# A transformer block on one core: where the row-sum fold, the row inverses and the two norms stand in a hand-written order of slots

## The chip, the cores and the metric

The kernel runs on one core of a Trainium2 chip. A core has a matrix engine (TensorE, PE in the profile; its weight loads are shown as PEld), a vector engine (VectorE, DVE), a scalar engine for activation functions and copies (ScalarE, ACT), a general engine (GpSimd, POOL) and a queue engine that here only issues transfers (SyncE, SP). Each engine works through its own instructions in order and waits for others by semaphores. ScalarE and GpSimd can issue transfers too, from within their own order of instructions. The metric is the time of one execution on the device in microseconds (us), the median of several runs.

## What is computed

The input x is 4 sequences of 1024 tokens with 512 features, with a condition vector of 128 values for each sequence. The block is a transformer layer with normalizations that are scaled and shifted by the condition:

```python
def _tc_rmsnorm(x, t, gw, gb, bw, bb):
    g = (t @ gw.T + gb)[:, None, :]
    b = (t @ bw.T + bb)[:, None, :]
    inv_rms = jax.lax.rsqrt(jnp.mean(x * x, axis=-1, keepdims=True) + EPS)
    return g * x * inv_rms + b
...
y = x + _attention(_tc_rmsnorm(x, t, g1w, g1b, b1w, b1b), Wq, Wk, Wv, Wo)
return x + (y + _swiglu(_tc_rmsnorm(y, t, g2w, g2b, b2w, b2b), gate_w, hid_w, out_w))
```

Attention has 16 heads of 32 features with a softmax over 1024 keys. swiglu is silu(x @ gate_w.T) * (x @ hid_w.T) @ out_w.T with 2048 hidden features. (The last lines put the reference's steps together; the names are the reference's.)

## The kernel before, in words

**Tiles.** Features lie on the 128 partitions (C = 4 chunks), tokens along the free dimension. A block n is 512 tokens (NBLK = 8 blocks; a sequence b is two of them, its halves). Attention is cut into groups j: one block, one chunk of four heads and 256 queries make one group, so a block has 8 groups and there are 64. A group has UN = 4 rounds r of 256 keys each.

**Slots.** Everything is in one loop over slots g, 0 to 267 (L758). A slot's kind is g % 4. Slot g computes the scores of round g (scores(), L301), copies them from PSUM (keep(), L308, tile raw) and takes the running maximum (L313, L316). The later steps of a round follow one group behind: in slot g, shifted() subtracts the row maximum from round g - 5 on VectorE (L354), exponential() follows on ScalarE (L357), and weighted() multiplies round g - 6 with the values on TensorE (L367, tile av), so it needs the exponential of the slot before. Accumulating transfers on GpSimd's queue add up the four rounds of a group for the row sums (L381). At kind 0 the maxima of the group before are transposed (max_T(), tile mt), reduced and split on VectorE (parts(), L328 to L333); at kind 1 they are transposed back (parts_T(), tile pt, then the copy mT on ScalarE, L340) and spread (spread(), L348 and L349, tile shift).

**Row sums and inverses.** fold_sum() (L389) adds the two halves of the accumulated exponentials on VectorE, 128x1024. It stands at the end of the kind 3 slot. sums() (L399) and the copy sums_out() (L404, tile total) follow in the next slot, kind 0. inverse() (L407) and normalize() (L416, which writes the tile oT) stand near the head of that group's kind 2 slot, ahead of shifted(). The product of a block's first group is put off to the kind 1 slot of the next group.

**The feed-forward part** joins at slot FS = 60 and is worked off by units p, one in two slots (p = (g - 60) // 2; 16 units for each block, with seven products of halves in place of eight). In the even slot: pair_26(), copy_156(), the contraction with the output weights of an earlier unit (filler(), tile pc), its addition to the residual take_contract() (L568), pair_7() and sub_5() (L537). In the odd slot: pair_3(), tanh (L547), pair_15() and take_5() (L511) of the next unit, gate() (L552), add_15() (L515), pair_4() and hidden() (L555). pair_26() of the next even slot writes the bank that add_15() has read. Until slot 60, projections for the later sequences (project_kq(), project_v()) fill the slots instead, one or two a slot, handed out by chain() from a queue in order. weight_sums() makes sums of feed-forward weights, four VectorE operations, in each third slot from 6 to 51.

**The norms.** The first norm of half a sequence that comes later: norm_squares() (squares on ScalarE, L132, sums on VectorE, L135 and L138), norm_root() (a matmul with ones over the partitions, tile pma, then the root from PSUM to SBUF, L146), a reciprocal on VectorE (L622), norm_scale() (L184) and norm_mod() (L187) for each chunk. Six of these run in the slots before 60; the root stands in the kind 0 slots 4, 12, 20, 28, 36 and 44. The second norm of block n, with g0 = 32 (n + 1), starts when project_out() (tile po, addition L435) has made x2. Its root is made in slot g0 + 17 on all 128x512 values (in every partition the same 512), and then one row is written to DRAM by norm_compact(), read back as 128x4 by take(), inverted there by invert() (L162), written out by put() and read to all partitions by norm_spread() (L173), which SP issues. compact(), take() and put() are issued by ScalarE. Then come norm_scale(), norm_mod() and token_sums() (L482 to L488), which prepares the sums for the feed-forward products. This goes for blocks 0 to 6; block 7 is normed at the end in another way.

**What sets the order.** The order on PE, DVE, ACT and POOL is the order in which the code calls the steps. SP's issues are ordered by the framework, and SP waits at each issue until its buffer is free. pin(g, ...) puts a load into slot g, between() puts a step near a slot's end (halfway), after() at its very end (ended), amid within an odd slot of the feed-forward part, behind take_5(). Scores use PSUM banks of their own; projections, row sums, means and spreads share two banks of the pool ps (tag w), with a third for each third projection (ps_b); av has its own bank (ps_av).

Of the kernel before, what the change touches and what calls it, by code (L numbers as in the profile page):

```python
# [10 lines left out]
F32 = mybir.dt.float32  # L11
BF16 = mybir.dt.bfloat16
AF = mybir.ActivationFunctionType
# [4 lines left out]
P = 128  # L18
NB = 512
# [5 lines left out]
def tile_cond_transformer_block(  # L25
# [24 lines left out]
    HQ = 256  # L50
# [77 lines left out]
    def norm_squares(dst, tag: str, k: int):  # L128

        sq = [sb.tile([P, NB], F32, tag="t", name=f"sq{tag}_{2 * k + i}", bufs=2) for i in range(2)]  # L130
        for i in range(2):
            nc.scalar.activation(sq[i], dst[:, 2 * k + i, :], AF.Square)  # L132
        if k == 0:
            state[tag] = sb.tile([P, NB], F32, tag="tot", name=f"tot{tag}", bufs=1)
            nc.vector.tensor_tensor(state[tag], sq[0], sq[1], ALU.add)  # L135
        else:
            for t in sq:
                nc.vector.tensor_tensor(state[tag], state[tag], t, ALU.add)  # L138

    def norm_root(tag: str, inside: bool = False):  # L140
        if inside:
            pm = ps_av.tile([P, NB], F32, tag="av", name=f"pm{tag}")
        else:
            pm = ps.tile([P, NB], F32, tag="w", name=f"pm{tag}")
        mm(pm, ones_mean, state[tag], True, True)
        nc.scalar.activation(state[tag], pm, AF.Sqrt, bias=eps)  # L146

    def compact(tag: str, t, rows: int, n: int):

        inv_s[tag] = tc.dram_tile([P // rows, n], F32, name=f"sums{tag}")  # L150
        nc.scalar.dma_start(out=inv_s[tag], in_=t[0:P:rows, :])

    def take(tag: str):

        src = inv_s.pop(tag)
        few = sb.tile([P, src.shape[0] * src.shape[1] // P], F32, tag="few", name=f"few{tag}", bufs=2)
        nc.scalar.dma_start(out=few, in_=src.rearrange("h (p c) -> (h p) c", c=few.shape[1]))
        state["few", tag] = few

    def invert(tag: str):  # L160
        few = state["few", tag]
# [2 lines left out]
    def put(tag: str):  # L164
        few = state.pop(("few", tag))
        inv_s[tag] = tc.dram_tile(list(few.shape), F32, name=f"invs{tag}")
        nc.scalar.dma_start(out=inv_s[tag], in_=few)

    def spread_inverse(tag: str, t, rows: int, n: int):

# [216 lines left out]
    def fold_sum(j: int):  # L387
        t = acc[j]
        nc.vector.tensor_tensor(t[:, 0, :, :], t[:, 0, :, :], t[:, 1, :, :], ALU.add)  # L389
# [16 lines left out]
    def inverse(j: int):  # L406
        nc.vector.reciprocal(state["total", j], state["total", j])  # L407
# [163 lines left out]


    NR = NBLK * C * (NB // HQ) * UN
    BS = C * (NB // HQ) * UN
    MS = BS // C
    pinned = {}
    first = deque()
# [35 lines left out]
    for b in range(1, B):  # L613
        for half in range(QB):
            s = math.ceil((len(queue) + 1) / PACE)
            s4 = s - 4 - (s - 6) % UN
            tag = f"a{b}_{half}"
            pin(max(s4 - 6, 0), load_y, b, half)
            for k in range(2):
                after(s4 - 4 + k, lambda b=b, half=half, tag=tag, k=k: norm_squares(y[b, half], tag, k))  # L620
            between(s4 - 2, norm_root, tag)
            after(s4 - 1, lambda tag=tag: nc.vector.reciprocal(state[tag], state[tag]))  # L622
            for c in range(C):
                between(s4, lambda b=b, half=half, tag=tag, c=c: norm_scale(y[b, half], tag, c))
                after(s4 + c // 2, lambda b=b, half=half, c=c: norm_mod(0, b, y[b, half], c))
            for load, fn, a in chains_of(b, half):
                enqueue(s, load, fn, a)
# [4 lines left out]
    for n in range(NBLK):  # L632
        g0 = (n + 1) * BS
        pin(g0 + 6, load_res, n)
        go = g0 + (13 if n < NBLK - 1 else 8)
        for d in range(C):
            first.append((go, None, project_out, (n, d)))
            pin(go - 3 + (d // 2 * 4 if n else 0), load_wo, n, d)
        if n < NBLK - 1:
            tag = f"f{n}"  # L640
            after(g0 + 16, add_res, n)
            for k in range(2):
                after(g0 + 15 + k, lambda n=n, tag=tag, k=k: norm_squares(x2[n], tag, k))
            if g0 + 17 < FS:
                between(g0 + 17, norm_root, tag)
            else:
                amid.setdefault(g0 + 17, []).append((norm_root, (tag, True)))
            between(g0 + 17, norm_compact, tag)
            after(g0 + 19, take, tag)
            between(g0 + 20, invert, tag)  # L650
            after(g0 + 21, put, tag)
            after(g0 + 22, norm_spread, tag)
            for c in range(C):
                after(g0 + 24 + c // 2, lambda n=n, tag=tag, c=c: norm_scale(x2[n], tag, c))
            for c in range(2):
                after(g0 + 25, lambda n=n, c=c: norm_mod(1, n // QB, x2[n], c))
            for c in range(2, C):
                between(g0 + 26, lambda n=n, c=c: norm_mod(1, n // QB, x2[n], c))
            for i in range(4):
                after(g0 + (26, 26, 27, 28)[i], token_sums, n, i)  # L660
    for m in range(NBLK * C):
        if m:
            for qh in range(NB // HQ):
# [24 lines left out]
    with tc.manual_schedule(  # L688
# [69 lines left out]
        while g < END:  # L758
# [17 lines left out]
                scores(g)  # L776
            if kind == 1 and m_on:
                spread(j_m, 0)

            if kind == 2 and n_on and j_n < direct:  # L780
                inverse(j_n)
                if j_n % (BS // UN):
                    normalize(j_n)
            if kind == 1 and n_on and j_n % (BS // UN) == 1:
                normalize(j_n - 1)
            if x_on and kind != 1:
                shifted(r_x)
            if late is not None:
# [17 lines left out]
            if not ffn:  # L806
# [20 lines left out]
                    add_15(0)  # L827
                elif even:
                    late = chain(g, FG)
                if kind == 3 and s_on:  # L830
                    fold_sum(j_s)
                if g in (FS - 4, FS - 2):
                    load_f((g - FS + 4) // 2)
            elif even:
# [22 lines left out]
            else:  # L857
# [27 lines left out]
                if kind == 1:  # L885
                    gate(p)
                    if evict is not None:
                        evict()
                if kind == 3 and s_on:
                    fold_sum(j_s)  # L890
                pair_4(p)
                hidden(p)
                if due:
                    chain(g)()
                for fn, a in halfway.pop(g, []):
                    fn(*a)
            columns[0] = DH
            for fn, a in ended.pop(g, []):
                fn(*a)
# [93 lines left out]
```

## Time and profile before

| | |
|---|---|
| time, median of 3 runs | 2498.34 us (2495.81 to 2498.56) |
| the profiled execution's own time | 2495.65 us |
| its span from first to last instruction | 2493.8 us |
| PE busy | 2392.5 us, 96% of the span |
| DVE busy | 1941.8 us, 78% |
| ACT busy | 1406.4 us, 56% |
| transfers | 501.69 MB, mean 201 GB/s |
| slots 0 to 59 | from 50 to 544 us |
| slots 60 to 255 | from 544 us on; slot 254 begins at about 2144 us |

How to read it: the profile shows one execution. A row such as "L354 DVE TENSOR_TENSOR raw<-raw,shift ... x320 | 594.1, 1857 | 101.7" gives the source line, the engine, the operation, what it writes from what, the shapes, how often, its busy time in us, the mean of one in ns, and the idle time of the engine just ahead of it. In a view in order of time, a line begins with its start and its length in us, and what stands in brackets at its end is how long the engine was idle ahead of it and which instruction ended that. In the view of waits a line names who waited for whom, the total in us, how often, and the longest. Matmuls are pipelined, so TensorE counts as busy also while one waits in its pipe; what counts are the gaps and the lengths of slots.

### The profile page before, as it was taken

What the parts mean: (1) busy time and instruction counts of PE and PEld (TensorE: products, weight loads), DVE (VectorE), ACT (ScalarE), POOL (GpSimd) and SP (SyncE); (2) the same over time, 40 slices, a digit from 0 to 9 for tenths busy, and PEclk for the clock granted to TensorE, in tenths of its full rate; (3) what the DMA queues carried; (4) which work ended last, traced back from release to release, by engine and by line L of the source; (5) the groups of instructions that cost most, each with busy time, mean ns of one, the idle gap of its engine ahead of it and who ended that gap; (6) DMA issues with size and microseconds to landing.
All of it is one profiled execution on the core that took longest, in us unless ns stands there. A gap on an engine that the chain in (4) does not pass through costs nothing. (4 is left out here: it accounts for less than half of the span.)

```text
span 2493.8 us, 71084 instructions
## 1 busy us (share of the span) xinstructions
PE 2392.5 (96%) x31749; PEld 1125.5 (45%) x31749; DVE 1941.8 (78%) x2180; ACT 1406.4 (56%) x1488; POOL 172.4 (7%) x207
## 2 busy tenths in 40 slices
PE   8999999999999999999999999999999999999999
PEld 3333333345444444444444444444444444444444
DVE  2688888878979997999789988998899979843332
ACT  3677667766656665666566656665666656522111
POOL 0000000000000000000000000000000000000000
PEclk9999999999999999999999999999999999999999
DMA  6698999888878898888878888889788978863442
GB/s 213 175 290 242 239 250 235 221 209 230 209 174 205 210 229 200 194 207 225 203 186 202 234 191 199 207 214 221 180 204 195 240 183 202 195 177 112 141 131 73
DMA packets 185982, 501.69 MB, mean 201 GB/s; under 512 B 21319, under 2 KB 78663, under 8 KB 158286
## 3 DMA queue, kind: packets, MB, share of 16 engines
q0 software_dynamic: 28656, 208.68, 42.7%
q1 hardware_dynamic: 154704, 288.42, 35.3%
q8 instruction: 250, 4.10, 0.6%
q10 hardware_dynamic: 2318, 0.05, 0.1%
q14 instruction: 54, 0.44, 0.1%
HBM read 246.44 MB, written 41.97 MB: 116 GB/s over the span
## 5 line engine op out<-in xcount | busy, mean ns | idle before, releaser
L354 DVE TENSOR_TENSOR raw<-raw,shift 128x2048 f32<-128x2048 f32 (+1 forms) x320 | 594.1, 1857 | 101.7 <-ACT shift L349 98.2
L357 ACT ACTIVATE raw<-raw 128x2048 f32<-128x2048 f32 x256 | 490.9, 1918 | 321.2 <-DVE raw L354 321.0
L308 ACT COPY raw<-sc 128x2048 f32<-128x2048 f32 x256 | 478.8, 1870 | 86.0 <-PE sc L301 44.0
L313 DVE TENSOR_TENSOR rmax<-rmax,raw 128x1024 f32<-128x1024 f32 x384 | 469.1, 1222 | 58.1 <-ACT raw L308 53.2
L106 PE MATMUL pc<-h,ow 128*32 128x512 f32 x4096 | 467.9, 593 | 2.3 <-ACT total L404 1.1
L367 PE MATMUL av<-raw,v 128*32 128x256 f32 x4096 | 274.1, 385 | 61.5 <-ACT raw L357 55.1
L381 POOL DMA_DIRECT2D raw<-raw x192 | 165.3, 861 | 2009.0 <-ACT raw L357 945.4
L301 PE MATMUL sc<-q,k 32*128 32x256 f32 x4096 | 293.3, 400 | 1.8 <-ACT raw L308 1.8
L106 PE MATMUL pa<-x,fa 128*32 128x256 f32 x4096 | 269.1, 380 | 8.1 <-DVE pa L515 8.0
L106 PE MATMUL pa<-sums,fw 128*32 128x256 f32 x4096 | 267.9, 379 | 0.0
L106 PEld LDWEIGHTS pc<-h,ow 128*32 128x32 f32 x4096 | 127.6, 110 | 246.5 <-issue 221.6
L301 PEld LDWEIGHTS sc<-q,k 32*128 32x128 f32 x4096 | 184.9, 184 | 117.8 <-issue 79.4
L106 PE MATMUL pkq<-y,wkq 128*32 128x512 f32 (+1 forms) x1664 | 231.6, 594 | 4.2 <-ACT y L187 4.1
L367 PEld LDWEIGHTS av<-raw,v 128*32 128x32 f32 x4096 | 106.9, 109 | 188.3 <-ACT raw L357 109.8
L106 PEld LDWEIGHTS pa<-x,fa 128*32 128x32 f32 x4096 | 127.5, 109 | 122.8 <-DVE pa L515 28.8
L106 PEld LDWEIGHTS pa<-sums,fw 128*32 128x32 f32 x4096 | 133.1, 110 | 87.9
L530 ACT COPY pb<-pa 128x256 f32<-128x256 f32 x128 | 46.3, 362 | 179.5 <-PE pa L106 174.9
L547 ACT ACTIVATE t<-pa 128x512 f32<-128x512 f32 x128 | 78.0, 609 | 119.7 <-PE pa L106 119.6
L106 PE MATMUL pa<-x,fw 128*32 128x256 f32 x2048 | 135.2, 381 | 0.0
L106 PE MATMUL pb<-x,fw 128*32 128x256 f32 x2048 | 134.0, 379 | 1.2 <-ACT pb L530 1.2
L106 PE MATMUL pb<-sums,fa 128*32 128x256 f32 x2048 | 134.0, 379 | 0.0
L106 PEld LDWEIGHTS pkq<-y,wkq 128*32 128x32 f32 (+1 forms) x1664 | 73.2, 116 | 131.5 <-issue 119.4
(104 smaller groups left out, 2166.0 us busy)
## 6 DMA issues: line engine op xcount, KB each, us to landing
raw<-raw POOLq DMA_DIRECT2D x192, 1024.0 KB, 9.2
fw<-sw SPq DMA_DIRECT2D x128, 512.0 KB, 5.8
fa<-in_gh_w SPq DMA_DIRECT2D x128, 384.0 KB, 7.8
ow<-in_out_w SPq DMA_DIRECT2D x128, 256.0 KB, 3.4
wkq<-in_kq_w SPq DMA_DIRECT2D x32, 512.0 KB, 9.1
v<-vs SPq DMA_DIRECT2D x128, 128.0 KB, 6.0
k<-kqs SPq DMA_DIRECT2D x124, 128.0 KB, 7.7
kqs<-st SPq DMA_DIRECT2D x61, 256.0 KB, 6.3
```

The source lines that it names most:

```text
L106: nc.tensor.matmul(dst[k : k + n, :], w[:, k : k + n], moving, start=start, stop=stop, skip_group_check=seeded)
L301: nc.tensor.matmul(sc[:, i, k, :], keys[rows, k * P : (k + 1) * P], queries[rows, :], start=True, stop=True)
L308: nc.scalar.copy(raw[r].rearrange("p k h q -> p h k q"), state.pop(("sc", r)))
L313: nc.vector.tensor_tensor(rmax[j], rmax[j], raw[r][:, k, :, :], ALU.max)
L354: nc.vector.tensor_tensor(t, t, s.unsqueeze(1).to_broadcast(list(t.shape)), ALU.add)
L357: nc.scalar.activation(raw[r], raw[r], AF.Exp)
L367: nc.tensor.matmul(av[j][i * DH : (i + 1) * DH, :], v[m, u][:, k, i * DH : (i + 1) * DH], raw[r][:, k, i, :], start=(kt == 0), stop=(kt == ...
L381: nc.gpsimd.dma_start(out=acc[j].rearrange("p k h q -> p (k h q)"), in_=raw[r].rearrange("p k h q -> p (k h q)"), accum_op=ALU.add,)
L530: nc.scalar.copy(bank_b[p][:, RIGHT], bank_a[p][:, RIGHT])
L547: nc.scalar.activation(state["t", p], bank_a[p], AF.Tanh, scale=0.5)
```

## The change

It moves steps to other places in the order; the arithmetic of the results is the same but for where the second norm's root is taken.

- fold_sum() goes from the end of the kind 3 slot to the head of the next slot, kind 0, ahead of shifted() (and so behind hidden() of the slot before).
- inverse() and normalize() go from the head of the kind 2 slot to its end, behind sub_5(). For a block's last group they stand at the end of the kind 0 slot. Only block 1's first product is still put off to kind 1.
- The first norm's load, squares, root and reciprocal come one slot sooner: the root at the end of kind 3, the reciprocal at the end of kind 0. Scaling stays where it was.
- The second norm of blocks 1 to 6 starts four slots sooner, with its output projection (slots g0 + 9 and g0 + 11 for g0 + 13 and g0 + 15) and the loads of its weights. Its mean is copied from PSUM in slot g0 + 13 instead of the root (norm_mean()), goes to DRAM and back as 128x4, and the root is taken there (root(), end of slot g0 + 16), with the inverse at the end of g0 + 17. The scalings stand at the ends of g0 + 22 (two chunks) and g0 + 24, the modulations in g0 + 23 and g0 + 25, the first token sum at the end of g0 + 25. Block 0 keeps its places, with the root at the end of slot 52 and norm_mean() in 49.
- compact(), take() and put() are issued by SP.

```diff
-    def norm_root(tag: str, inside: bool = False):
+    def norm_root(tag: str):
...
+    def norm_mean(tag: str, inside: bool):
...
-        nc.scalar.activation(state[tag], pm, AF.Sqrt, bias=eps)
+        nc.scalar.copy(state[tag], pm)
...
-        nc.scalar.dma_start(out=inv_s[tag], in_=t[0:P:rows, :])
+        nc.sync.dma_start(out=inv_s[tag], in_=t[0:P:rows, :])
...
-        nc.scalar.dma_start(out=few, in_=src.rearrange("h (p c) -> (h p) c", c=few.shape[1]))
+        nc.sync.dma_start(out=few, in_=src.rearrange("h (p c) -> (h p) c", c=few.shape[1]))
...
+    def root(tag: str):
+        few = state["few", tag]
+        nc.scalar.activation(few, few, AF.Sqrt, bias=eps)
...
-        nc.scalar.dma_start(out=inv_s[tag], in_=few)
+        nc.sync.dma_start(out=inv_s[tag], in_=few)
...
-            pin(max(s4 - 6, 0), load_y, b, half)
+            pin(max(s4 - 7, 0), load_y, b, half)
             for k in range(2):
-                after(s4 - 4 + k, lambda b=b, half=half, tag=tag, k=k: norm_squares(y[b, half], tag, k))
-            between(s4 - 2, norm_root, tag)
-            after(s4 - 1, lambda tag=tag: nc.vector.reciprocal(state[tag], state[tag]))
+                after(s4 - 5 + k, lambda b=b, half=half, tag=tag, k=k: norm_squares(y[b, half], tag, k))
+            between(s4 - 3, norm_root, tag)
+            after(s4 - 2, lambda tag=tag: nc.vector.reciprocal(state[tag], state[tag]))
...
-        go = g0 + (13 if n < NBLK - 1 else 8)
+        e = g0 if n == 0 else g0 - 4
+        go = e + 13 if n < NBLK - 1 else g0 + 8
...
-            after(g0 + 16, add_res, n)
+            after(e + 16, add_res, n)
             for k in range(2):
-                after(g0 + 15 + k, lambda n=n, tag=tag, k=k: norm_squares(x2[n], tag, k))
-            if g0 + 17 < FS:
-                between(g0 + 17, norm_root, tag)
+                after(e + 15 + k, lambda n=n, tag=tag, k=k: norm_squares(x2[n], tag, k))
+            if n == 0:
+                between(e + 17, norm_mean, tag, False)
             else:
-                amid.setdefault(g0 + 17, []).append((norm_root, (tag, True)))
-            between(g0 + 17, norm_compact, tag)
-            after(g0 + 19, take, tag)
-            between(g0 + 20, invert, tag)
-            after(g0 + 21, put, tag)
-            after(g0 + 22, norm_spread, tag)
+                amid.setdefault(e + 17, []).append((norm_mean, (tag, True)))
+            after(e + 17, norm_compact, tag)
+            after(e + 19, take, tag)
+            after(e + 20, root, tag)
+            after(e + (20 if n == 0 else 21), invert, tag)
+            after(e + (21 if n == 0 else 22), put, tag)
+            after(e + (22 if n == 0 else 24), norm_spread, tag)
+            scales, mods = ((24, 24, 25, 25), (25, 25, 26, 26)) if n == 0 else ((22, 22, 24, 24), (23, 23, 25, 25))
             for c in range(C):
-                after(g0 + 24 + c // 2, lambda n=n, tag=tag, c=c: norm_scale(x2[n], tag, c))
-            for c in range(2):
-                after(g0 + 25, lambda n=n, c=c: norm_mod(1, n // QB, x2[n], c))
-            for c in range(2, C):
-                between(g0 + 26, lambda n=n, c=c: norm_mod(1, n // QB, x2[n], c))
+                after(g0 + scales[c], lambda n=n, tag=tag, c=c: norm_scale(x2[n], tag, c))
+                between(g0 + mods[c], lambda n=n, c=c: norm_mod(1, n // QB, x2[n], c))
             for i in range(4):
-                after(g0 + (26, 26, 27, 28)[i], token_sums, n, i)
+                after(g0 + (26, 26, 27, 28)[i] - (n > 0 and i == 0), token_sums, n, i)
...
-            if kind == 2 and n_on and j_n < direct:
-                inverse(j_n)
-                if j_n % (BS // UN):
-                    normalize(j_n)
-            if kind == 1 and n_on and j_n % (BS // UN) == 1:
-                normalize(j_n - 1)
+            if kind == 0 and n_on:
+                fold_sum(j_n)
+            if kind == 1 and j_n == GB + 1:
+                normalize(GB)
...
-                if kind == 3 and s_on:
-                    fold_sum(j_s)
...
+            if kind == 0 and n_on and j_n < direct and j_n % GB == GB - 1:
+                inverse(j_n)
+                normalize(j_n)
+            if kind == 2 and n_on and j_n < direct and j_n % GB != GB - 1:
+                inverse(j_n)
+                if j_n != GB:
+                    normalize(j_n)
```

More of the change, by code (lines that the diff above doesn't have):

```diff
@@ L138, in norm_squares @@
                 nc.vector.tensor_tensor(state[tag], state[tag], t, ALU.add)
-    def norm_root(tag: str, inside: bool = False):
+    def norm_root(tag: str):
+        pm = ps.tile([P, NB], F32, tag="w", name=f"pm{tag}")
+        mm(pm, ones_mean, state[tag], True, True)
+        nc.scalar.activation(state[tag], pm, AF.Sqrt, bias=eps)
+    def norm_mean(tag: str, inside: bool):
         if inside:
@@ L573, in tile_cond_transformer_block @@
     NR = NBLK * C * (NB // HQ) * UN
-    BS = C * (NB // HQ) * UN
+    GB = C * (NB // HQ)
+    BS = GB * UN
     MS = BS // C
@@ L888, in tile_cond_transformer_block @@
                         evict()
-                if kind == 3 and s_on:
-                    fold_sum(j_s)
                 pair_4(p)
```

## The prediction, made before the changed kernel was run

> **What bounds the kernel now.** I read the busy times, then who waits for whom on TensorE before and after 544 us (slot 60, where the feed-forward part joins), then stretches of single groups, then the order in time of each engine. Slots, kinds and groups are those explained above: slot g, kind g mod 4, group of four slots.
>
> ```profile
> PE 2392.5 (96%) x31749; PEld 1125.5 (45%) x31749; DVE 1941.8 (78%) x2180; ACT 1406.4 (56%) x1488; POOL 172.4 (7%) x207
> ```
> TensorE is busy nearly throughout. The change removes no matmul, so it can win only TensorE's idle time, some 100 us. Before 544 us, TensorE's own waits are (us in total, times, longest):
> ```profile
> PE av L367 <- ACT raw L357: 17.1, 15, 2.4
> PE pma L106 <- ACT total L404: 7.6, 5, 1.7
> PE sc L301 <- ACT raw L308: 1.8, 3, 1.0
> PE sp L348 <- ACT shift L349: 0.7, 1, 0.7
> ```
> That is 27.2 us in the front. It hangs on the first norm, once per half sequence, as around slots 28 to 30:
> ```profile
> 281.53 1.13 PE L106 MATMUL pma<-tota,ones_mean 128*128 128x512 f32 x2 [1.66 <-ACT total L404]
> ...
> 294.74 1.07 PE L367 MATMUL av<-raw,v 128*32 128x256 f32 x16 [1.30 <-ACT raw L357]
> ```
> ```profile
> 291.49 1.28 ACT L357 ACT_TABLE_LOAD   x1
> ```
> ```profile
> 288.14 2.55 DVE L354 TENSOR_TENSOR raw<-raw,shift 128x1024 f32<-128x1024 f32 x2 [4.96 <-ACT shift L349]
> ...
> 293.63 3.35 DVE L622 RECIPROCAL tota<-tota 128x512 f32<-128x512 f32 x1
> ```
> The mean's matmul waits for the row sums' bank; the root's table must be swapped back just before the exponential that weighted() needs (1.30 us); and the 3.35 us reciprocal stands in the busy slot 30, while DVE idles 4.96 us in slot 29.
>
> In the feed-forward part a group without extras takes 30.50 us, one with the second norm's root 33.90, one with its scaling 33.10:
> ```profile
> 1010.30:1040.80 30.50, 30.01 (x439) 15.13 (x439) 27.70 (x32) 19.14 (x20) 2.58 (x3) 1.00 0.87 217
> 712.60:746.50 33.90, 31.17 (x451) 15.17 (x443) 27.04 (x32) 23.73 (x25) 1.75 (x3) 1.00 0.74 170
> 777.00:810.10 33.10, 30.08 (x439) 15.13 (x439) 31.35 (x37) 21.81 (x24) 2.58 (x3) 1.00 0.87 202
> ```
> (After the length stand PE, PEld, DVE, ACT and POOL busy.) In the plain group TensorE's 30.01 us fall 0.49 short, and VectorE says why:
> ```profile
> 1027.60 1.74 DVE L407 RECIPROCAL total<-total 128x256 f32<-128x256 f32 x1
> 1029.38 0.42 DVE L416 TENSOR_TENSOR oT<-avs,total 128x256 f32<-128x256 f32 x1
> 1029.72 2.28 DVE L354 TENSOR_TENSOR raw<-raw,shift 128x2048 f32<-128x2048 f32 x1
> ...
> 1040.32 0.42 DVE L515 TENSOR_TENSOR pa<-pa,p 128x256 f32<-128x256 f32 x1
> 1040.65 1.21 DVE L389 TENSOR_TENSOR raw<-raw 128x1024 f32<-128x1024 f32 x1
> ```
> ```profile
> 1034.00 1.07 PE L367 MATMUL av<-raw,v 128*32 128x256 f32 x16 [0.30 <-ACT raw L357]
> 1040.80 0.42 PE L106 MATMUL pa<-x,fa 128*32 128x256 f32 x4 [0.19 <-DVE pa L515]
> ```
> From slot 117 to add_15 at 1040.32 VectorE has no gap. pair_26 waits for that add; so from kind 1 to kind 3 every us of VectorE counts, and from pair_26 to the next kind 1 TensorE sets the pace.
>
> [...]the exponential starts 1.29 us after the load[...] The norm's 2 KB transfers land only after 6.7 to 9.1 us here; I use those. [...]
>
> **Part 1, first norm one slot sooner.** (a) The mean now comes at the end of a kind 3 slot. In the built program its bank is the one of the previous slot's first projection, long evicted: the 7.6 us go. In slot 11 its matmuls also fall under a wait of 0.98 for the scores' bank: 0.9 more. (b) The exponential's table is reloaded in kind 0, where ScalarE idles 2.94 us at 279.31 ahead of it: five waits of 1.30 go (6.5). The reciprocal goes to the end of kind 0. There DVE has finished the parts at 283.2; without the 1.66 us wait the next shift would come at 286.5, so 3.35 us just fit. In slots 12 and 36 weight_sums() (4 x 0.35 us) follows it: there the shift, and so weighted(), comes 1.35 us late, twice 1.35 given back. Net 3.8. (c) With 3.35 us gone from kind 2, the waits that follow the scaling (slots 8, 16, 23, 24, 32, 40, 47, 48: 0.7+0.5+1.3+1.0+2.4+1.0+1.5+1.6 = 10.0) shrink. After slot 29 at its start + 7.5: shift 2.2, maxima 2.4, scaling 2.4, row inverse and product 2.1, weight_sums 1.4, shift 2.25, exponential 2.0: + 22.4, against + 21.7 where TensorE wants it: 0.7 stays, so in slots 24 and 32; in 48 the output projection's adds leave 1.5. Net 7.1. The squares come a slot sooner too; their input lands at about 123 us, asked for at 125: nothing.
>
> **Part 2, second norm of block 0.** Its root falls at the end of kind 0 (slot 52), its reload before the just-in-time exponential of slot 53, as at 291.49: +1.3. Before, root and reload sat in slot 50, where nothing waited. Front: -7.6 - 0.9 - 3.8 - 7.1 + 1.3 = -18.1.
>
> **Part 3, second norm of blocks 1 to 6, per block.** Root group: the mean leaves a copy (0.59, the row of st<-pkq) in place of load, root and load (1.28+0.69+1.28). The copy stands ahead of the tanh that gate() needs, so VectorE is 0.5 late; TensorE's mean with its wait for the av bank (0.86+0.2) takes the slack: 31.1 in place of 33.9, -2.8. Next group: the root on 128x4 and its load go into ScalarE's idle 2.27 us before mT; the reload before slot g0+17's exponential costs 1.28, and invert() now stands in kind 1, 0.2: +1.5. Next: two scalings at the end of kind 2, 2 x 0.6: +1.2. Next: token sums at the ends of kinds 1 and 2, 1.2, in place of 2.6 (two scalings and two sums): -1.4; the third sum's 0.4 in the following slot stays. The other scalings and the last sum sit in VectorE's 1.5 us gap of kind 1, free as at 785.3. Sum -1.5, x6 = -9.1. The output projection is moved four slots with its loads; those groups are TensorE-bound (43.84 of 43.90).
>
> **Part 4, row sums in each group.** Inverse and product pass behind sub_5 but stay ahead of add_15: VectorE's chain is as long as before. weighted() no longer waits 0.30, pair_26 waits 0.49 for 0.19: nothing won. The fold passes from behind add_15 to behind hidden(), and now ends at about 1011.96 in the group where the sums' matmul starts at 1012.05: ready only just. Bounds 0 and 0.1 us per group (a late weight load); I take 0.05 x 46 = +2.3.
>
> **Part 5, DMAs from ACT's queue to SP's.** 21 issues, under 0.4 us each. On SP, the take waits for its predecessor's landing (7 to 9 us), the spread likewise; behind them stand ow, q, k, fw and fa loads. SP already stood still 8.5 us before the spread (761.2 to 769.6), and slots 87 and 88 were normal. The loads behind have their buffers free only in the next slot: 0, at most one slot's delay per block. few lands 13.4 to 18.2 us after the copy; the root has 21.4 us.
>
> Sum: -18.1 - 9.1 + 2.3 = -24.9. The profiled execution took 2495.65 (span 2493.8), so 2470.7; the median shown is 2.7 higher: 2473.
>
> **Rivals.** (1) The group's own moves pay: if weighted()'s 0.30 us is really won in 46 groups (13.8) and the fold costs nothing (2.3), 2457. For: the wait is there each time; against: VectorE's unbroken chain. (2) Only the front pays: reload, lone scalings and fold eat part 3, or the reciprocal doesn't fit in kind 0: about 2482. (3) Slower: root() waits in ScalarE's queue for few; if the two landings took over 21 us, the row maxima's copy mT behind it stops TensorE. In seven blocks 3.6 us each eat the gain; at two landings of 15 us it is 8.6 each, 60 in all: 2533. Against: 6.7 to 9.1 measured. That the order isn't moved at all is excluded: the built program has it.
>
> **Numbers.** Forecast 2473: 0.60; rival 1: 0.12; rival 2: 0.20; rival 3 and like mishaps: 0.08. Below 2460 and above 2487 I leave about a tenth each. Measurement tells 0.2% (5 us) from no change. Faster 0.88 (all of the first two cases and most of rival 2), same 0.05, slower 0.07.
>
> **What would show it.** No pma wait and none of 1.30 in slots 22, 30, 46, but one in 54; the 3.35 us reciprocal right behind the parts of the maxima at the end of kind 0; plain groups still 30.5; the root group 31.1 with no table load in it, the next about 32; the root on 128x4 without a wait for its DMA. Plain groups at 30.0 would be rival 1; a wait of mT's engine for few, rival 3.

## The result, and the profile after

The changed kernel takes 2478.86 us (median of four runs, 2478.3 to 2480.0) against 2497.4 for the kernel before (2495.8 to 2498.6): the ratio is 0.9927, with a 95% interval from 0.9910 to 0.9944. That is 18.5 us less; the forecast was 24.9 less, 2473 us, with a range of 2460 to 2487. The profiled executions are 2495.65 us before and 2480.0 after; the changed kernel's profile is of its longest run, and the other three took 0.6 to 1.7 us less.

Every line number below that belongs to the changed kernel is nine or ten higher than that of the same statement before: shifted() is L363, exponential() L366, weighted() L376, fold_sum() L398, inverse() L416, normalize() L425, sub_5() L546, take_contract() L577.

I read the two traces by one mark, the start of each slot's scores. It cuts the execution into four stretches (us; the last is the span less the start of slot 254):

| stretch | before | after | difference | forecast |
|---|---|---|---|---|
| start, up to slot 0 | 50.0 | 50.6 | +0.6 | 0 |
| front, slots 0 to 59 | 494.0 | 477.0 | -17.0 | -18.1 |
| feed-forward part, slots 60 to 253 | 1599.7 | 1597.4 | -2.3 | -6.8 |
| end, from slot 254 | 350.1 | 353.1 | +3.0 | 0 |

First the page's busy times. TensorE's share rises by one point, no more:

```profile
PE 2396.0 (97%) x31785; PEld 1121.8 (45%) x31785; DVE 1943.7 (78%) x2180; ACT 1412.4 (57%) x1495; POOL 172.4 (7%) x207
```

Then TensorE's waits in the front (total, times, longest). The mean's wait for its bank, 7.6 us before, is gone, and the wait of weighted() fell from 17.1 to 10.2:

```profile
PE av L376 <- ACT raw L366: 10.2, 10, 1.8
PE sp L357 <- ACT shift L358: 0.7, 1, 0.7
PE pma L106 <- DVE tota L138: 0.3, 1, 0.3
```

VectorE's order in time at slot 28 (start, length, then the wait ahead in brackets) shows the reciprocal right behind the parts of the maxima, with the next shift following it at once:

```profile
277.91 0.18 DVE L342 SCALAR_TENSOR_TENSOR split<-top,split 128x8 bf16<-128x8 f32 x1
277.99 3.35 DVE L632 RECIPROCAL tota<-tota 128x512 f32<-128x512 f32 x1
281.25 2.29 DVE L363 TENSOR_TENSOR raw<-raw,shift 128x1024 f32<-128x1024 f32 x2
```

Third, five groups of block 1 in the feed-forward part: with the mean, with the root, with the first scalings, with the last ones, and a plain one (length, then PE, PEld, DVE, ACT and POOL busy):

```profile
674.53:706.11 31.58, 31.11 (x448) 15.22 (x446) 29.09 (x33) 21.40 (x22) 1.72 (x2) 1.00 0.81 204
706.11:738.13 32.02, 30.12 (x440) 15.06 (x438) 27.78 (x32) 20.61 (x20) 2.60 (x3) 1.00 0.85 201
738.13:769.88 31.75, 30.05 (x440) 15.06 (x438) 28.83 (x33) 20.53 (x21) 2.59 (x3) 1.00 0.82 197
769.88:802.25 32.37, 30.22 (x441) 15.06 (x439) 30.63 (x36) 20.54 (x21) 2.58 (x3) 1.00 0.79 193
832.91:863.46 30.55, 30.05 (x440) 15.06 (x438) 27.63 (x31) 19.21 (x19) 2.58 (x3) 1.00 0.76 185
```

Last, the wait of a plain group. The 0.30 us of weighted() went from kind 3 to kind 0, and pair_26 waits 0.20 behind it. Together they are the 0.5 us of before; the forecast had the same sum, but all of it at pair_26:

```profile
854.18 1.07 PE L376 MATMUL av<-raw,v 128*32 128x256 f32 x16 [0.30 <-ACT raw L366]
855.45 1.07 PE L106 MATMUL pa<-x,fa 128*32 128x256 f32 x16 [0.20 <-DVE pa L524]
```

So the front and the plain groups went nearly as forecast. What is missing is in the groups with extras and at the end. My theory for the experiments: the norms pay what I reckoned, and the moved row sums and inverses (part 4) cost more than the 2.3 us I gave them. The rival: these moves carry part of the front's gain, and the second norm is the part that falls short.

### The profile page after: what moved, and what is told of

Its sections match the earlier page's. It is cut to its first block, busy times and chain, and to the rows that moved or that the text cites. A ratio compares the mean times of both kernels' runs of the same rounds, so it can differ in the third digit from the quotient of the medians.

```text
span 2478.1 us, 71138 instructions
## 1 busy us (share of the span) xinstructions
PE 2396.0 (97%) x31785; PEld 1121.8 (45%) x31785; DVE 1943.7 (78%) x2180; ACT 1412.4 (57%) x1495; POOL 172.4 (7%) x207
## 5 line engine op out<-in xcount | busy, mean ns | idle before, releaser
L363 DVE TENSOR_TENSOR raw<-raw,shift 128x2048 f32<-128x2048 f32 (+1 forms) x320 | 593.9, 1859 | 65.2 <-ACT shift L358 62.3
L366 ACT ACTIVATE raw<-raw 128x2048 f32<-128x2048 f32 x256 | 490.8, 1917 | 214.3 <-DVE raw L363 213.8
L322 DVE TENSOR_TENSOR rmax<-rmax,raw 128x1024 f32<-128x1024 f32 x384 | 469.5, 1223 | 53.9 <-ACT raw L317 48.2
L376 PE MATMUL av<-raw,v 128*32 128x256 f32 x4096 | 274.9, 386 | 50.0 <-ACT raw L366 50.0
L376 PEld LDWEIGHTS av<-raw,v 128*32 128x32 f32 x4096 | 107.2, 109 | 175.8 <-ACT raw L366 88.0
L577 DVE SCALAR_TENSOR_TENSOR res<-pc,res 128x512 f32<-128x512 f32 x128 | 88.2, 689 | 67.2 <-PE pc L106 62.9
```

The costliest lines, as they stand in the source:

```text
L322: nc.vector.tensor_tensor(rmax[j], rmax[j], raw[r][:, k, :, :], ALU.max)
L363: nc.vector.tensor_tensor(t, t, s.unsqueeze(1).to_broadcast(list(t.shape)), ALU.add)
L366: nc.scalar.activation(raw[r], raw[r], AF.Exp)
L376: nc.tensor.matmul(av[j][i * DH : (i + 1) * DH, :], v[m, u][:, k, i * DH : (i + 1) * DH], raw[r][:, k, i, :], start=(kt == 0), stop=(kt == ...
L577: nc.vector.scalar_tensor_tensor(r, pp, 0.5, r, ALU.mult, ALU.add)
```

## The experiments

Medians in us, with lowest and highest, and the ratio to the kernel before run on the same chip, with its 95% interval:

| kernel | median | ratio |
|---|---|---|
| first_norm_alone | 2480.70 (2480.46 to 2481.18) | 0.9935 (0.9923 to 0.9948) |
| second_norm_alone | 2488.12 (2486.53 to 2488.71) | 0.9963 (0.9950 to 0.9975) |
| row_moves_alone | 2511.59 (2507.35 to 2514.92) | 1.0055 (1.0041 to 1.0069) |
| no_row_moves | 2472.55 (2470.99 to 2473.22) | 0.9900 (0.9885 to 0.9915) |
| inverse_back | 2473.35 (2473.31 to 2474.24) | 0.9905 (0.9889 to 0.9922) |
| fold_back | 2476.19 (2474.76 to 2476.36) | 0.9914 (0.9900 to 0.9929) |
| end_mended | 2476.67 (2475.63 to 2481.62) | 0.9925 (0.9912 to 0.9937) |
| root_at_full_width | 2484.08 (2483.97 to 2484.65) | 0.9946 (0.9933 to 0.9958) |
| small_transfers_on_scalar_queue | 2476.62 (2476.57 to 2478.38) | 0.9919 (0.9905 to 0.9932) |
| product_in_kind1 | 2448.83 (2448.32 to 2449.27) | 0.9806 (0.9791 to 0.9821) |
| root_before_exponential | 2441.49 (2439.79 to 2442.63) | 0.9774 (0.9761 to 0.9787) |
| root_and_weight_sums | 2438.51 (2437.51 to 2440.82) | 0.9764 (0.9751 to 0.9777) |

### Each part by itself

**first_norm_alone** is the kernel before with these lines only:

```diff
-            pin(max(s4 - 6, 0), load_y, b, half)
+            pin(max(s4 - 7, 0), load_y, b, half)
-                after(s4 - 4 + k, ... norm_squares ...)
+                after(s4 - 5 + k, ... norm_squares ...)
-            between(s4 - 2, norm_root, tag)
-            after(s4 - 1, ... reciprocal ...)
+            between(s4 - 3, norm_root, tag)
+            after(s4 - 2, ... reciprocal ...)
```

> The kernel before with the first norm one slot sooner and nothing else. Own theory: the gain in front of slot 60 is this shift alone; TensorE's waits for the mean (7.6 us), for the reloaded exponential and after the scalings shrink as in the changed kernel, and the wait of 1.29 us in slot 54 is not there: about 18 us less than before, 2479 us, with the groups of the feed-forward part and the end as before. Rival: the moved row sums and inverses relieve the kind 0 and kind 2 slots and carry part of the front; then this kernel gains only 8 to 12 us, 2486 to 2490, and waits of 1 to 2.4 us after the scalings (slots 23, 24, 32, 47) stay.

Measured: 16.5 us less than the kernel before, where my theory had 18. The front is 478.0 us (16.0 less), the feed-forward part 1600.4 and the end 350.0, both as before. The waits of slots 23 and 47 are gone, those of slots 24 and 32 are 0.61 each. The front's gain is this shift. The trace also shows what my sum left out: in slots 20 and 44 weighted() waits 1.22 us, where two adds of the squares (0.69 each) now stand ahead of the shift in kind 3, and in slot 35 0.92, where the first add, weight sums and an inverse stand ahead of the shift in kind 2.

**second_norm_alone** is the changed kernel with the first norm, the fold and the inverse where they were; only a block's last inverse stays at the end of kind 0.

> The changed kernel with the first norm, the fold and the inverse put back where they were; only a block's last inverse stays at the end of kind 0, as the earlier output projection needs it. Own theory: 0.75 us per block less in blocks 1 to 6 (4.5 in all), 1.3 more in slot 54: 3 us less than before, 2494, and the end as long as before. Rival: the second norm depends on the moved inverse; with the inverse back at the head of kind 2 the late root and scalings cost the same 1.3 to 1.5 us each and nothing is left: 2497 to 2499.

Measured: 9.1 us less, three times what my theory said and against the rival too. The feed-forward part is 1590.1 us, 9.6 less than before, where the whole change gains only 2.3. The group with the mean takes 30.99 us, not 31.58. (The front is 2.1 us longer: TensorE's waits there sum to 0.7 more, and a stretch behind a wait of 2.45 us in slot 32, in which TensorE runs at half its clock, makes up the rest; the last section has more on it.) So the second norm pays as in the prediction (9.1), and something else in the change takes it away.

**row_moves_alone** is the kernel before with these lines:

```diff
-            if kind == 2 and n_on and j_n < direct:
-                inverse(j_n)
-                ...
+            if kind == 0 and n_on:
+                fold_sum(j_n)
...
-                if kind == 3 and s_on:
-                    fold_sum(j_s)
...
+            if kind == 2 and n_on and j_n < direct:
+                inverse(j_n)
+                ...
             columns[0] = DH
```

> The kernel before with the row sums' fold at the head of kind 0 and the inverse and product at the end of kind 2, both norms as before. Own theory: no gain in the front; plain groups 30.55 for 30.50 us (0.05 x 46 = 2.3) and the end 3.0 us longer, because in the last group's kind 3 slot the inverse (1.74 + 0.42 us) stands ahead of the shift that weighted() needs: 5 us more than before, 2502 to 2503. Rival: the moves free VectorE where the front waits, 5 to 9 us less there: 2494 to 2498.

Measured: 14.4 us more than before: front +7.3, feed-forward part +6.4, end +2.1. No theory had a loss in the front. VectorE's order there shows it: behind the first norm's scalings (L184) the inverse and the product are in the way of the shift that weighted() waits for.

```profile
234.59 1.89 DVE L184 TENSOR_TENSOR y<-y,tota 128x512 f32<-128x512 f32 x3
236.40 1.75 DVE L407 RECIPROCAL total<-total 128x256 f32<-128x256 f32 x1
238.18 0.42 DVE L416 TENSOR_TENSOR oT<-avs,total 128x256 f32<-128x256 f32 x1
238.52 2.29 DVE L354 TENSOR_TENSOR raw<-raw,shift 128x2048 f32<-128x2048 f32 x1
```

TensorE then waits 2.55 us, and pays again behind the wait: the same 16 matmuls that take 1.07 us elsewhere take 1.94.

```profile
242.80 1.94 PE L367 MATMUL av<-raw,v 128*32 128x256 f32 x16 [2.55 <-ACT raw L357]
244.51 4.36 PE L106 MATMUL pkq<-y,wkq 128*32 128x512 f32 x32
```

Slots 24, 28 and 32 each show such a half-speed stretch. They are the larger part: TensorE's waits in the front sum to 28.6 us for 27.2 before, so some 6 of the 7.3 us are matmuls at half speed. The feed-forward part has three more such stretches, behind waits of 1.93 us in slots 124, 188 and 220. The three parts by themselves sum to 16.5 + 9.1 - 14.4 = 11.2 us less, the whole change has 18.5 less. With the first norm shifted, its reciprocal of 3.35 us is out of the kind 2 slots; the inverse then has its place behind the scalings, and the loss in the front isn't there: 477.0 us with the moves, 478.1 without them (no_row_moves, below).

### Which move costs

**no_row_moves** is the changed kernel with fold and inverse back; **inverse_back** and **fold_back** put back one of the two:

```diff
 inverse_back and no_row_moves, ahead of shifted():
+            if kind == 2 and n_on and j_n < direct and j_n % GB != GB - 1:
+                inverse(j_n)
+                if j_n != GB:
+                    normalize(j_n)
 fold_back and no_row_moves, at the end of kind 3:
+                if kind == 3 and s_on:
+                    fold_sum(j_s)
```

> The changed kernel with fold and inverses where they were before (a block's last inverse stays at the end of kind 0); both norms as changed. Own theory, from the two norms run alone: the moved inverses cost about 7 us in the feed-forward part and 3 at the end and gave 2 in the front, so this kernel takes 8 us less than the changed one, 2470 to 2472; the root's group falls from 31.58 to 30.99 us. Rival: the moves cost only with the old first norm and pay with the new one; then this kernel is as long as the changed one, 2477 to 2480, or longer.

> The changed kernel with only the inverse and product back at the head of kind 2; the fold stays at the head of kind 0. Own theory: the inverse, not the fold, carries the loss, because behind the maxima it leaves VectorE waiting for TensorE's last sums in groups with extras and then stands ahead of the next shift: 2472 to 2474, plain groups 30.55, root's group near 31.0, the end as in the kernel before. Rival: the fold at the head of kind 0 delays the shift there and carries the loss: 2477 to 2480.

> The changed kernel with only the fold back at the end of kind 3, behind add_15; the inverses stay moved. Own theory: the fold alone costs 0.05 us per group, the late weight load: plain groups 30.50 and 1 to 3 us less, 2476 to 2478, the root's group still near 31.6. Rival (the fold carries the loss): 2470 to 2473 and the root's group near 31.0.

Measured: 6.3, 5.5 and 2.7 us less than the changed kernel, the first 0.5 us above what my theory expected, the others inside it; the rivals fall, all three. Inverse and fold add up to 8.2, a little more than both at once. Groups of block 1, in the order of the fence above (us):

| kernel | mean | root | scalings | last scalings | plain |
|---|---|---|---|---|---|
| changed | 31.58 | 32.02 | 31.75 | 32.37 | 30.55 |
| fold_back | 31.54 | 31.98 | 31.72 | 32.17 | 30.51 |
| inverse_back | 31.04 | 32.02 | 31.75 | 32.36 | 30.55 |
| no_row_moves | 30.99 | 31.98 | 31.71 | 32.17 | 30.51 |

Two clean effects: the fold costs 0.04 to 0.05 in every group (in the plain one the weight load of the row sums starts 0.03 us ahead of its matmul, 857.19 for 857.22; in the kernel before it was 0.22, 1011.83 for 1012.05) and 0.2 where scalings crowd it; the inverse costs 0.54, and of these five only in the group with the mean. VectorE's order in the changed kernel says how:

```profile
687.80 1.22 DVE L322 TENSOR_TENSOR rmax<-rmax,raw 128x1024 f32<-128x1024 f32 x1
689.15 0.69 DVE L577 SCALAR_TENSOR_TENSOR res<-pc,res 128x512 f32<-128x512 f32 x1
690.08 0.43 DVE L546 TENSOR_TENSOR pb<-pb,p 128x256 f32<-128x256 f32 x1 [0.24 <-PE pb L106]
690.42 1.74 DVE L416 RECIPROCAL total<-total 128x256 f32<-128x256 f32 x1
692.20 0.43 DVE L425 TENSOR_TENSOR oT<-avs,total 128x256 f32<-128x256 f32 x1
692.54 2.28 DVE L363 TENSOR_TENSOR raw<-raw,shift 128x2048 f32<-128x2048 f32 x1
```

and in no_row_moves:

```profile
683.78 1.74 DVE L416 RECIPROCAL total<-total 128x256 f32<-128x256 f32 x1
685.56 0.43 DVE L425 TENSOR_TENSOR oT<-avs,total 128x256 f32<-128x256 f32 x1
685.90 2.29 DVE L363 TENSOR_TENSOR raw<-raw,shift 128x2048 f32<-128x2048 f32 x1
688.10 2.48 DVE L322 TENSOR_TENSOR rmax<-rmax,raw 128x1024 f32<-128x1024 f32 x2
690.50 0.68 DVE L577 SCALAR_TENSOR_TENSOR res<-pc,res 128x512 f32<-128x512 f32 x1
691.10 0.42 DVE L546 TENSOR_TENSOR pb<-pb,p 128x256 f32<-128x256 f32 x1
```

In this group TensorE has the mean on top (1.07 us) and is late with the sums that take_contract() and sub_5() read. With the inverse in front of them, VectorE works through that time without a gap. With the inverse behind them, VectorE first stands still for them (0.13 ahead of L577, 0.24 ahead of L546) and then makes the next shift wait for the 2.1 us of inverse and product. In the plain group TensorE isn't late, and the order costs nothing.

### The end

**end_mended** changes the changed kernel only in the slots without scores:

```diff
                 shifted(r_x)
+            if kind == 3 and g > NR and n_on and j_n < direct:
+                inverse(j_n)
+                normalize(j_n)
...
-            if kind == 2 and n_on and j_n < direct and j_n % GB != GB - 1:
+            if kind == 2 and g < NR and n_on and j_n < direct and j_n % GB != GB - 1:
```

> The changed kernel, but in the slots after the last scores the inverse and product stand behind the shift of the kind 3 slot. Own theory: TensorE's wait of 2.56 us in the last kind 0 slot shrinks below 0.5 and the matmuls behind it that took 1.93 and 1.88 us take 1.07 again: 3 to 4 us less than the changed kernel, 2475 to 2476. Rival: the wait is set by the exponential alone, which comes as late with either order, so 0 to 1 us less, 2478 to 2479.

Measured: 2.2 us less in the median than the changed kernel, between the two, and with two of its five runs as long as 2481. The means differ by only 0.8 us and the intervals of the two ratios overlap, so the times alone don't show a gain; the traces show where one is made and lost. In the changed kernel the inverse and the product of group 61 stand ahead of a shift that has no scores to cover it:

```profile
2163.04 1.74 DVE L416 RECIPROCAL total<-total 128x256 f32<-128x256 f32 x1
2164.81 0.42 DVE L425 TENSOR_TENSOR oT<-avs,total 128x256 f32<-128x256 f32 x1
2165.16 2.28 DVE L363 TENSOR_TENSOR raw<-raw,shift 128x2048 f32<-128x2048 f32 x1
```

The kind 0 slot behind it has the wait and the half speed:

```profile
2169.44 1.93 PE L376 MATMUL av<-raw,v 128*32 128x256 f32 x16 [2.56 <-ACT raw L366]
2171.14 1.88 PE L106 MATMUL pa<-x,fa 128*32 128x256 f32 x16
```

In end_mended the wait is 0.44 and both runs of matmuls take 1.07:

```profile
2168.22 1.07 PE L376 MATMUL av<-raw,v 128*32 128x256 f32 x16 [0.44 <-ACT raw L366]
2169.34 1.07 PE L106 MATMUL pa<-x,fa 128*32 128x256 f32 x16
```

The wait and the half speed are two things. The kernel small_transfers_on_scalar_queue (below) has the same order here and the same wait, but no half speed:

```profile
2168.64 1.07 PE L376 MATMUL av<-raw,v 128*32 128x256 f32 x16 [2.56 <-ACT raw L366]
2169.53 1.05 PE L106 MATMUL pa<-x,fa 128*32 128x256 f32 x16
```

From the start of slot 254 to the contraction (pc) that follows, it takes 48.2 us there, 49.8 in the changed kernel, 47.2 in the kernel before and 46.3 in end_mended. So the moved inverse itself costs 1.0 us here, and half speed, where it follows, 1.6.

What end_mended saves can be lost behind it: the last group's sums wait for the accumulating transfer of the exponentials, whose landing varies:

```profile
2195.08 1.23 DVE L398 TENSOR_TENSOR raw<-raw 128x1024 f32<-128x1024 f32 x1 [3.43 <-DMA raw<-raw]
```

That wait is 1.11 us before, 1.03 after, 3.43 here, and there is none in small_transfers_on_scalar_queue. In this profiled execution it gave the saving back, together with a second stretch at half speed behind it. The moved inverse is one cause of the longer end, then, and the smaller one; the rest depends on the transfer and on TensorE's clock. The end shows it: 350.4 us in small_transfers_on_scalar_queue with the inverse moved, 352.8 in no_row_moves with the inverse back, where half speed came behind waits of 1.44 and 0.65 us. Over all kernels it lies between 349.9 and 353.8 us.

### The root, the queue, and two further versions

**root_at_full_width** takes the root of the second norm at once on 128x512 (norm_root in place of norm_mean in blocks 1 to 6, no root() later):

> The changed kernel, but in blocks 1 to 6 the root is taken at once on the 128x512 mean, as before, still four slots sooner; the inverse stays on distinct values. Own theory: the two table loads and the root stand again in front of gate_tanh() in the mean's group, which goes from 31.6 to about 34.2; the next group falls from 32.0 to 30.6: about 1.1 more per block, 2484 to 2488. Rival: what counts is only the place four slots sooner; 2477 to 2481.

Measured: 2484.1, 5.2 us more than the changed kernel, at the edge of what my theory gave. The group with the mean goes to 33.95, the next from 32.02 to 30.94 (30.62 in block 2). So the root on distinct values is worth about one us per block, and not the wait it removes (2.4): 1.28 of it comes back as the reload in the next group.

**small_transfers_on_scalar_queue** issues the three 2 KB transfers from ScalarE's queue again, as before:

> The changed kernel with the second norm's three small transfers issued from ScalarE's queue again. Own theory: which queue issues them costs nothing, 2477 to 2481. Rival: 21 issues of 0.4 us, or ScalarE waiting for a landing of 7 to 9 us in each of seven blocks, show: 2487 and more.

Measured: 2476.6, no loss. Both kernels have 1597.4 us in the feed-forward part and 477.0 in the front; the profiled executions differ at the start (0.8 us) and at the end (2.7 us) alone. The queue costs nothing, as the prediction said.

**product_in_kind1** builds on no_row_moves and asks whether VectorE's chain really sets a plain group:

```diff
-                if j_n != GB:
-                    normalize(j_n)
-            if kind == 1 and j_n == GB + 1:
-                normalize(GB)
+            if kind == 1 and n_on and 0 < j_n <= direct and j_n % GB:
+                normalize(j_n - 1)
```

> As no_row_moves, but a group's product (0.42 us) is made at the head of the following kind 1 slot, where VectorE stands still 1.6 us. Own theory: in the feed-forward part VectorE's unbroken chain from kind 1 to add_15 sets a group's 30.50 us; 0.42 us out of it give 30.1 us, some 44 times: 16 to 18 us less than no_row_moves, 2453 to 2456. Rival: ScalarE's exponential or TensorE stands right behind VectorE, a plain group stays above 30.4, and the time is within 4 us of no_row_moves.

Measured: 2448.8, 23.7 us less than no_row_moves and more than my theory's 16 to 18. The profiled executions differ by 24.3 us: 20.4 in the feed-forward part (1569.9 for 1590.3), 1.1 in the front and 2.9 at the end, where no_row_moves had its half speed. The product stands in VectorE's pause of kind 1, and a plain group takes 29.98 us, of which TensorE is busy 29.93:

```profile
826.47 0.41 DVE L425 TENSOR_TENSOR oT<-avs,total 128x256 f32<-128x256 f32 x1
828.20 2.49 DVE L363 TENSOR_TENSOR raw<-raw,shift 128x1024 f32<-128x1024 f32 x2 [1.31 <-ACT shift L358]
```

```profile
826.14:856.12 29.98, 29.93 (x440) 15.16 (x438) 27.46 (x31) 19.32 (x19) 2.58 (x3) 1.00 0.81 182
701.87:733.33 31.46, 30.01 (x440) 15.15 (x438) 27.61 (x32) 20.69 (x20) 2.60 (x3) 1.00 0.80 194
```

The gain per group is 0.53 us where 0.42 were taken out: both waits of TensorE go, and the groups with scalings gain as much.

**root_before_exponential** moves the root ahead of the exponential of a kind 2 slot, in the pause of ScalarE there:

```diff
-            after(e + 20, root, tag)
+            if n == 0:
+                after(e + 20, root, tag)
+            else:
+                early.setdefault(e + 22, []).append((root, (tag,)))
```

> As product_in_kind1, but in blocks 1 to 6 the root stands two slots later, ahead of the kind 2 exponential, where ScalarE stands still 2.8 us; inverse and put follow in the next slot. Own theory: root, its table load and the exponential's reload (0.30 + 1.28 + 1.28 = 2.86 us) fit that gap to 0.1 us, so the wait of 1.28 us in the slot that followed the root goes: that group 30.2 for 31.46, six times 1.2: 7 us less than product_in_kind1, 2441 to 2443. Rival: the reload only changes its place and delays the kind 2 exponential by its length: no gain, 2447 to 2450.

Measured: 2441.5, 7.3 us less. ScalarE does load, root and reload in one row, and the exponential starts 7.22 us into its slot, 0.15 later than in a plain group of product_in_kind1:

```profile
712.85 0.36 ACT L539 COPY pb<-pa 128x256 f32<-128x256 f32 x1 [0.47 <-PE pa L106]
713.23 1.28 ACT L167 ACT_TABLE_LOAD   x1
714.52 0.30 ACT L167 ACTIVATE fewf<-fewf,eps 128x4 f32<-128x4 f32 x1
714.84 1.28 ACT L366 ACT_TABLE_LOAD   x1
716.13 1.92 ACT L366 ACTIVATE raw<-raw 128x2048 f32<-128x2048 f32 x1
```

The group takes 29.98 us, as a plain one does, where product_in_kind1 has 31.46.

**root_and_weight_sums** changes one line, and tests the term for the reciprocal in slots 12 and 36:

```diff
-        after(3 * f + 6, weight_sums, f, 1)
+        after(3 * f + 6 + (f in (2, 10)), weight_sums, f, 1)
```

> As root_before_exponential, and the two weight sums that stood behind the first norm's reciprocal (slots 12 and 36) stand one slot later, where VectorE idles. Own theory: the waits of 1.34 and 1.68 us in slots 14 and 38 shrink below 0.4: 2 to 3 us less than root_before_exponential. Rival: the reciprocal alone already fills the end of kind 0, or the sums delay kind 1 as much: within 1 us of it.

Measured: 2438.5, 3.0 us less. The wait in slot 14 is gone, that in slot 38 is 0.21, and the front is 2.5 us shorter. This is the best kernel of the study: 59 us less than before, 40 less than the changed one.

## Why the prediction was right, and where it was not

The measured 2478.9 us lie inside the range and 5.9 us above the forecast of 2473: the parts on the two norms held, the part on row sums and inverses did not.

**Front, -18.1 forecast, -17.0 measured.** Term by term from the waits of TensorE slot by slot. The mean's wait for its bank: all 7.6. Slot 11: -0.5 for -0.9, since the mean waits 0.3 for its squares there. The exponential's reload: waits of 1.30 gone in slots 22, 30 and 46, kept as 1.34 in slots 14 and 38: -3.8 for -3.8, and root_and_weight_sums shows that weight_sums() behind the reciprocal was the reason for the two that stayed. After the scalings: -7.3 for -7.1. Block 0's root: +1.29 in slot 54 for +1.3.

Not in my sum: slots 12, 20 and 36 wait 1.1, 0.55 and 0.55 us more, 2.2 together. The squares' adds moved into kind 3 slots as well, ahead of the shift, and where weight sums (slot 19) or an inverse (slot 35) stand there too, it comes late. The step that missed it is "The squares come a slot sooner too; their input lands at about 123 us, asked for at 125: nothing": it looked at the squares' input and not at their adds on VectorE. These terms sum to -15.7; the other 1.3 us are TensorE's busy time (465.4 us for 466.6), and what shortened it stays open. That the front came so near is luck in part: in no_row_moves, without the moved inverse, the adds cost 3.5 us in slots 12, 20, 35 and 36, and the inverse, which I had put at nothing in the front, took 1.3 of it away. Two sums are off by little: the terms behind slot 29 add up to 22.25, not 22.4, so 0.55 stays for 0.7 (measured 0.61), and six times 1.5 is 9.0, not 9.1.

**Second norm, blocks 1 to 6, -9.1 forecast.** Second_norm_alone measures -9.6 in the feed-forward part. In no_row_moves the groups differ from before by -2.9, +1.5, +1.2 and -1.4 (33.91, 30.50, 30.50 and 33.56 before); forecast were -2.8, +1.5, +1.2 and -1.4. This part of the working held in every term.

**Row sums and inverses, +2.3 forecast.** The fold is right: inverse_back minus no_row_moves in the feed-forward part is 1592.7 - 1590.3 = 2.4 us. The failed step is "Inverse and product pass behind sub_5 but stay ahead of add_15: VectorE's chain is as long as before", which I took from a plain group and let stand for all. It holds in the plain group (30.55 with, 30.55 without). It fails where TensorE is late, in the group with the mean: 0.54 us in six blocks, 3.2 of the 4.2 us by which fold_back is longer than no_row_moves there. The other 1.0 us lies in single groups, the first two of the part above all, and I haven't followed it. And the step fails at the end, which I never looked at: behind the last scores the inverse stands ahead of the last kind 3 shift, TensorE waits 2.56 us where it waited 1.45, and the next contraction comes 1.0 us later; the half speed that followed in the profiled execution added 1.6.

**Part 5, 0 forecast.** Small_transfers_on_scalar_queue shows no cost of the queue. My 7 to 9 us for a landing was too long: at the new places the inverse lands after 3.3 us on SP's queue (median of 7) and 4.1 on ScalarE's, which changed nothing. SP did wait for the landings, 13.2 us in seven takes (2.0 at most) and 13.9 in seven spreads (3.6 at most).

**The rivals.** "The group's own moves pay" is out: plain groups stayed at 30.55. "Only the front pays" describes the time (2482 for 2479) but not the cause: the reload and the scalings cost what was reckoned, and the moved inverse took back part of it. Root() never waited for its transfer, so the slower rival is out too: in the timeline its table load starts 0.02 us after the exponential.

## What to carry to other kernels

A chain of an engine that shows no gap in one kind of iteration can have gaps in others; before costing a reorder at nothing, check the iterations with extras and the last ones, and ask which moved step was filling the time until a late input came. Work that nobody waits for belongs into a pause that the engine has anyway: 0.42 us moved into VectorE's pause of kind 1 gave 23.7 us, more than the whole change. A table switch cost time here only where the next function was due: the reload cost 1.28 us per block just ahead of an exponential that was waited for, and nothing where root and both loads fit a pause of 2.9 us.

## What the runs showed of the hardware

**Half speed behind a wait.** Behind some of its waits TensorE runs at half its clock. In the changed kernel's end, behind a wait of 2.56 us, the granted clock was 0.50 for 3.36 us, and the matmuls, which start in groups of four, started 427 ns from group to group in place of 216. Here are the wait and two stretches behind it, with the granted clock third from the end:

```profile
2166.88:2169.40 2.52, 0.00 (x0) 0.00 (x0) 1.16 (x2) 1.93 (x2) 0.00 (x0) 1.00 1.10 186
2169.44:2172.80 3.36, 3.36 (x32) 1.55 (x36) 3.12 (x4) 0.20 (x1) 0.86 (x1) 0.50 0.59 187
2172.80:2176.00 3.20, 2.70 (x40) 1.02 (x36) 2.43 (x2) 1.96 (x3) 0.00 (x0) 0.99 0.99 267
```

Of the eleven waits of 2.4 to 3.1 us for exponentials or banks in all runs, seven were followed by slow matmuls; 2.44 us in slot 32 of the kernel before were not, 2.45 us in the same slot of second_norm_alone were. Of six waits of 1.93 us in row_moves_alone, one every 32 slots from slot 92 on, three were followed by them, as in slot 188:

```profile
1610.94 1.58 PE L367 MATMUL av<-raw,v 128*32 128x256 f32 x16 [1.93 <-ACT raw L357]
1612.28 1.95 PE L106 MATMUL pa<-x,fa 128*32 128x256 f32 x16
```

At the end of no_row_moves 1.44 and 0.65 us close together were followed by it; 1.52 and 0.65 in root_before_exponential were not. The wait of 2.56 us cost 4.2 in the changed kernel's end, half speed included (1.6), and 2.56 in small_transfers_on_scalar_queue, where none followed. What decides between the two, no run here shows.

**A table switch took its load and no more.** In root_before_exponential copy, load, root, load and exponential follow within 0.01 to 0.02 us of each other; the load's 1.28 us is the whole price here. In the changed kernel the root's load starts 0.02 us after the exponential ahead of it (703.93 us), and the root 0.01 us after its load.
